# Units of picks that run on from batch to batch, and a clamp of the messages' weights into PSUM, in a graph layer's kernel

## The chip, the cores and the metric

The kernel runs on one core of a Trainium2 chip. The time is device time of one execution, in microseconds; smaller is better. Before the change three runs took 1995.0, 2001.13 and 2002.62 us, with a median of 2001.13. The profile is of another execution, which took 2019.47 us, 2017.7 of them between its first and its last instruction.

## What is computed

One layer of a graph network with residual and normalization. `x` holds 6250 nodes of 64 values, and there are 206250 directed edges, sorted by their destination (the last 6250 by origin are loops).

```python
Qh = (x @ Wq.T + bq).reshape(n, H, D)          # H = 4 heads of D = 16
Kh = (x @ Wk.T + bk).reshape(n, H, D)
Vh = (x @ Wv.T + bv).reshape(n, H, D)
Ee = (edge_attr @ We.T + be).reshape(-1, H, D)
score = (Kh[src] * Qh[dst] * (1.0 / np.sqrt(D)) * Ee).sum(-1)
score = jnp.exp(jnp.clip(score, -5.0, 5.0))
msg = Vh[src] * score[..., None]
wV = jax.ops.segment_sum(msg, dst, num_segments=n)
x = _layernorm(x + wV.reshape(n, H * D), axis=-1)
```

## The kernel before

**Groups and steps.** The edges are cut in 1612 tiles of 128, and eight tiles are a group: 202 groups, whose loop (L1014 to L1139) is the kernel's main part. Two groups are a step. A group passes through stages that lie up to four groups ahead of it in the program:

- `edges(g + 3)`: TensorE multiplies the edges' attributes with We into the PSUM tile `ee`; `biased(g + 2)`: ScalarE adds the bias and makes `eb` in SBUF.
- `onehot_rows` makes one-hot columns of the destinations on ScalarE (`to`); `queries(g + 2)` multiplies them with rows of Q into the PSUM bank `qq`; `terms(g + 1)` is VectorE's product of `eb` and `qq`; `turn(g + 1)` are four transposes on TensorE (L775) into `qe`, of which there are two banks.
- `products(g)`: VectorE multiplies K of the sources with `qe` (`prod`) and reduces to `score`; `weigh(g)`: two ScalarE instructions take the exponential (`weight`); `message(g)`: VectorE multiplies `max(weight, LEAST)` with V of the sources, in one scalar_tensor_tensor (L830), whose product overwrites the group's bank `qe`.
- `keep` and `take` cut the message in two parts for exactness, the one on ScalarE, the other on VectorE (L850). `onehot_edges` (L792) compares destinations with a range, once in a step. `sums` multiplies both on TensorE into the PSUM region `pa`, and `add` (L900 to L909) reduces it on VectorE and adds the result to a ring of blocks. `fold_blocks` and `add_blocks` (L957) bring finished blocks from the ring to `y`.

`ee`, `pa` and `folded` are parts of one PSUM tile of two banks, called `room`; `ee` is its first bank, and the others share its second.

**Gathered and picked sources.** K and V of the sources come from a table in memory, 128 rows at a time, by GpSimd's indirect DMA (L295, 1260 of them). For the last two tiles of some groups, the PICKED ones, TensorE takes the rows of `x` out of `parts`, an SBUF copy of `x`, instead. This goes in 78 batches of four tiles. For a batch, 13 **units** of 512 nodes each run through TensorE: `picks` issues four matmuls a unit into the two banks `px` (tile names pick), with a one-hot tile `hot` that VectorE makes (L696). One-hots are made for two units together, a **piece**; those of pieces 1, 3 and 5 are made in bf16 (`thin`) and widened by ScalarE (`widened`, L707). The sums over units stay in the two banks until the last unit. Then `picked` takes the one wanted row of each four, with two VectorE instructions (L722, L723) that read `odd` (from the loaded `srcs`) and the banks and write `x` in SBUF (`xs`). The first pick of the next batch overwrites the banks, so it has to wait for both. In the next group, `biased_kv` sets the bank `qq` to the bias (ScalarE), `picked_kv` multiplies `x` with the weights of K and V into it (16 matmuls qq<-w,x), and `place_kv` copies it to the gathered rows' places (ScalarE, L739). `queries(g + 2)` of that group uses the same bank and is last in it, after `place_kv`.

**What sets the order.** Each engine runs its instructions in the order in which the loop issues them, and a tile framework adds the waits. Before the change batches take three and two groups by turns (LENGTHS), and `pieces_of` deals the seven pieces of a batch to its groups: 4, 4 and 5 units, or 6 and 7. The last group of a batch is its READY group: 3, 5, 8, 10, 13, and so on. In it, `picked` is the last thing but the closing of blocks. One-hots of a group's units are made in the group before (`ahead`). `sources` (which makes `odd` and the compared numbers from `srcs`) and `fetch_sources` (SyncE's load of `srcs`) run for the next batch at a batch's first group and for the one after in the group ahead.

```python
def picks(m, p, u):
    lo, hi = PIECES[p]
    for k in range(2):
        for part in range(2 if u < UNITS - 1 else 1):
            product(px[k], parts[:, u, part, 2 * k:2 * k + 2].rearrange("p t c -> p (t c)"),
                    HOT[m, p][:, u - lo, :], start=u == 0 and part == 0, stop=u == UNITS - 1)
```

## Time and profile before

| | us | share of the span |
|---|---|---|
| median of three runs | 2001.13 | |
| the profiled execution | 2019.47 | |
| its span | 2017.7 | |
| TensorE busy with matmuls | 1738.5 | 86% |
| VectorE busy | 1486.0 | 74% |
| ScalarE busy | 1328.1 | 66% |
| GpSimd busy | 1255.5 | 62% |
| matmuls of picks (3900) | 1143.6 | 57% |
| DMA, mean rate | 101 GB/s | |

In rows of the profile PE is TensorE, PEld its weight loads, DVE VectorE, ACT ScalarE, POOL GpSimd and SP SyncE. A tile is named by the program, and the number of a line is that of the file before (above). All matmuls but the transposes go through one helper and have its line, L744; they are told apart by the tile that they write. The granted clock of TensorE, in tenths over 40 slices of the span, stands at 9 for the most part, with single slices at 8:

```profile
PEclk9789999999999998999899999999989999999996
```

Busy shares are means over the whole span, start and end among them. They say which engine has the most to do, not which one is waited for; that is read from the waits and the chain.

### The profile page before, as it was taken

What the parts mean: (1) busy time and instruction counts of PE and PEld (TensorE: products, weight loads), DVE (VectorE), ACT (ScalarE), POOL (GpSimd) and SP (SyncE); (2) the same over time, 40 slices, a digit from 0 to 9 for tenths busy, and PEclk for the clock granted to TensorE, in tenths of its full rate; (3) what the DMA queues carried; (4) which work ended last, traced back from release to release, by engine and by line L of the source; (5) the groups of instructions that cost most, each with busy time, mean ns of one, the idle gap of its engine ahead of it and who ended that gap; (6) DMA issues with size and microseconds to landing.
All of it is one profiled execution on the core that took longest, in us unless ns stands there. A gap on an engine that the chain in (4) does not pass through costs nothing.

```text
span 2017.7 us, 25692 instructions
## 1 busy us (share of the span) xinstructions
PE 1738.5 (86%) x7993; PEld 1259.1 (62%) x7993; DVE 1486.0 (74%) x2650; ACT 1328.1 (66%) x2047; POOL 1255.5 (62%) x1310
## 2 busy tenths in 40 slices
PE   6569989888888898979888989888888988889995
PEld 6346666666666665657566666666666666656664
DVE  5457777777777686878777777778777777678786
ACT  3456676676766676767667667667766667577674
POOL 6566666666666665666666666666666666666441
PEclk9789999999999998999899999999989999999996
DMA  6523333333333333333333333333333333333320
GB/s 178 190 90 114 100 103 103 98 97 100 93 108 101 91 102 88 102 115 99 93 97 92 107 104 93 104 90 103 101 88 114 104 95 104 97 93 98 97 71 20
DMA packets 116116, 203.70 MB, mean 101 GB/s; under 512 B 54784, under 2 KB 56425, under 8 KB 115855
## 3 DMA queue, kind: packets, MB, share of 16 engines
q1 hardware_dynamic: 73932, 116.94, 19.0%
q0 software_dynamic: 41600, 83.97, 14.7%
q10 hardware_dynamic: 436, 1.04, 0.2%
q8 instruction: 65, 1.06, 0.2%
q14 instruction: 83, 0.68, 0.1%
HBM read 194.25 MB, written 7.59 MB: 100 GB/s over the span
## 4 chain that ended last, share of the span: by engine, by line
PE 63%; DVE 16%; issue 7%; ACT 6%; another core or an unknown queue 4%; DMA 2%; POOL 1%; DVEq 0%; SPq 0%; ACTq 0%; POOLq 0%
PE pick L744 37%; PE room L744 10%; PE qq L744 10%; PE qe L775 4%; DVE hot L696 3%; DMA kv<-kv_tab,src_i 2%; DVE score L808 2%; DVE prod L806 1%; DVE qe L830 1%; DVE x L722 1%; DVE term L769 1%; POOL kv L295 1%; ACT kv L739 1%; DVE msg L850 1%
## 5 line engine op out<-in xcount | busy, mean ns | idle before, releaser
L295 POOL DMA_INDIRECT kv<-kv_tab,src_i x1260 | 1216.2, 965 | 708.8 <-issue 277.1
L744 PE MATMUL pick<-hot,parts 128*128 128x512 f32 x3900 | 1143.6, 436 | 115.5 <-DVE x L722 79.5
L744 PEld LDWEIGHTS pick<-hot,parts 128*128 128x128 f32 x3900 | 742.3, 198 | 418.8 <-issue 167.8
L696 DVE TENSOR_TENSOR hot<-from,still 128x1024 fp32r<-128x1024 bf16 x231 | 280.3, 1213 | 0.6 <-ACT from L257 0.6
L707 ACT ACTIVATE hot<-thin 128x1024 fp32r<-128x1024 bf16 x234 | 245.4, 1049 | 19.4 <-remote 19.3
L769 DVE TENSOR_TENSOR term<-eb,qq 128x512 f32<-128x512 f32 x202 | 137.3, 680 | 137.2 <-PE qq L744 98.1
L755 ACT ACTIVATE eb<-room,be_col 128x512 f32<-128x512 f32 x202 | 137.1, 679 | 148.2 <-DVE still L900 50.4
L744 PE MATMUL room<-et,we_sb 128*128 128x512 f32 x404 | 226.2, 642 | 7.5 <-ACT eb L755 6.2
L844 ACT ACTIVATE msg<-qe 128x512 fp32r<-128x512 f32 (+1 forms) x206 | 123.2, 598 | 157.5 <-DVE qe L830 74.4
L278 ACT ACTIVATE to<-to,one_p 126x1024 bf16<-126x1024 bf16 x198 | 225.7, 1140 | 0.1
L272 ACT ACTIVATE to<-kb,minus_row 126x1024 bf16<-126x1024 uint8 x198 | 225.2, 1137 | 0.0
L813 ACT ACTIVATE score<-score,five_p 128x32 f32<-128x32 f32 x203 | 64.1, 316 | 235.4 <-DVE score L808 144.6
L775 PE MATMUL qe<-ident,term 128*128 128x128 f32 x806 | 135.5, 294 | 58.9 <-DVE term L769 39.4
L775 PEld LDWEIGHTS qe<-ident,term 128*128 128x128 f32 x806 | 104.0, 151 | 111.9 <-DVE term L769 55.8
L744 PE MATMUL qq<-w,x 128*128 128x128 f32 x1248 | 165.8, 288 | 5.0 <-issue 3.6
L806 DVE TENSOR_TENSOR prod<-kv,qe 128x512 f32<-128x512 f32 x203 | 137.0, 675 | 43.1 <-remote 38.3
L830 DVE SCALAR_TENSOR_TENSOR qe<-weight,kv 128x512 f32<-128x512 f32 x200 | 139.8, 699 | 35.1 <-ACT weight L815 22.3
L722 DVE SCALAR_TENSOR_TENSOR x<-odd,upper,pick 128x512 f32<-128x512 int32 x77 | 57.3, 744 | 144.7 <-PE pick L744 115.2
L744 PEld LDWEIGHTS qq<-w,x 128*128 128x128 f32 x1248 | 155.6, 202 | 12.9 <-issue 8.0
L696 DVE TENSOR_TENSOR thin<-from,still 128x1024 bf16<-128x1024 bf16 x231 | 157.1, 680 | 0.0
L808 DVE TENSOR_REDUCE score<-prod 128x32 f32<-128x512 f32 x203 | 138.5, 682 | 7.0
L850 DVE TENSOR_TENSOR msg<-qe,msg 128x512 fp32r<-128x512 f32 x194 | 132.2, 681 | 2.9 <-ACT msg L844 1.4
(166 smaller groups left out, 1490.5 us busy)
## 6 DMA issues: line engine op xcount, KB each, us to landing
et<-in_eT SPq DMA_DIRECT2D x100, 512.0 KB
kb<-key_tab SPq DMA_DIRECT2D x101, 252.0 KB
kv<-kv_tab,src_i POOLq DMA_INDIRECT x1260
srcs<-in_src_rows SPq DMA_DIRECT2D x78, 256.0 KB
qw<-q_tab SPq DMA_DIRECT2D x202, 15.8 KB
kv_tab<-kv_sb SPq DMA_DIRECT2D x4, 640.0 KB
q_tab<-q SPq DMA_DIRECT2D x5, 480.0 KB
out<-y SPq DMA_DIRECT2D x2, 512.0 KB
```

What stands on the lines that cost most here:

```text
L272: nc.scalar.activation(TO[g][:, :n, :], KB.pop(g)[:, :n * P].rearrange("p (j e) -> p j e", j=n), AF.Square, bias=minus_row3[:3 * W])
L278: nc.scalar.activation(TO[g][:, :n, :], TO[g][:, :n, :], AF.Relu, bias=one_p[:3 * W], scale=-1.0)
L295: return nc.gpsimd.indirect_dma_start(out=kv_of(g)[:, j, :], out_offset=None, in_=kv_tab[:, :], in_offset=bass.IndirectOffsetOnAxis(ap=src ...
L696: nc.vector.tensor_tensor(to.rearrange("p b (a c) -> p b a c", c=2), pairs((FROM if hi < UNITS else OVER)[m])[:, None].to_broadcast(shape) ...
L707: nc.scalar.activation(*THIN.pop(0), AF.Copy)
L744: mark.append(nc.tensor.matmul(*aps, **kw))
L769: nc.vector.tensor_mul(TERM[g][:, :n], EB.pop(g)[:, :n], qq[:, :n])
L775: nc.tensor.transpose(qe[g % 2][:, 2 * k:2 * k + 2, :], TERM[g][:, k, :], ident)
L806: nc.vector.tensor_mul(prod, kv_of(g)[:, lo:hi, :C], qe[g % 2][:, lo:hi, :])
L808: nc.vector.tensor_reduce(SCORE[g], prod.rearrange("p g (h d) -> p g h d", h=H), axis=AX.X, op=OP.add)
L830: nc.vector.scalar_tensor_tensor(to.rearrange("p g (h d) -> p g h d", h=H), WEIGHT.pop(g)[:, :, :, None].to_broadcast([P, n, H, D]), LEAST ...
L850: nc.vector.tensor_sub(part_of(g, 1)[1], left, part)
```

## The change

**Units.** A table FLOW gives the units of each five groups, 4, 6, 6, 4, 6, that is 26, two batches. A batch's units are now one stream, and a READY group has the last units of its batch (`head`, two or five of them) and then the first four or the first one of the next. Where the head is two units, they are issued early in the group, with `picked` right behind them. Where it is five, they come at the usual place, and `picked` follows edges. In both kinds of group `queries`, `sums` and `edges` come between the old batch's last units and the next one's first; `turn` does too in the first kind, and stands behind the second unit in the other. The group after READY has four units always. `sources` and `fetch_sources` run a group earlier.

**Clamp.** `message` is now a tensor_scalar that writes `max(weight, LEAST)` to `least_`, 32 columns of the PSUM bank `still`, and a tensor_tensor that multiplies with it from there.

**The tile room.** `ee` becomes a tile of its own, and `room` keeps `pa` and `folded`.

```diff
+FLOW = 4, 6, 6, 4, 6
+STREAM = [(m, p, u) for m in range(LAST) for p, piece in enumerate(PIECES) for u in range(*piece)]
+UPTO = [0] * (LEAD + 1)
+for g in range(LEAD, NG):
+    UPTO.append(UPTO[-1] + FLOW[(g - LEAD) % len(FLOW)] + (g == LEAD))
...
+def units_of(g):
+
+    return STREAM[UPTO[g]:UPTO[g + 1]] if g < NG else []
...
 def pieces_of(g):
...
+    return [(m, p) for m, p, u in units_of(g) if u == PIECES[p][0]]
...
+SOURCES = {LEAD: 1, **{r: m + 2 for m, r in enumerate(READY)}}
+FETCHES = {r - 1: m + 2 for m, r in enumerate(READY)}
...
-            room = fixed.tile([P, 2, 4 * P], F32, name="room")
-            ee = room[:, 0].rearrange("p (i e) -> p i e", e=P)
-            pa = room[:, 1, :2 * PA]
...
+            ee = fixed.tile([P, G // 2, P], F32, name="ee")
+            room = fixed.tile([P, 4 * P], F32, name="room")
+            pa = room[:, :2 * PA]
...
+            least_ = still[:, 3 * P:3 * P + G * H].rearrange("p (g h) -> p g h", h=H)
...
-                nc.vector.scalar_tensor_tensor(
+                nc.vector.tensor_scalar(least_[:, :n], WEIGHT.pop(g), LEAST, None, op0=OP.max)
+                nc.vector.tensor_tensor(
                     to.rearrange("p g (h d) -> p g h d", h=H),
-                    WEIGHT.pop(g)[:, :, :, None].to_broadcast([P, n, H, D]), LEAST,
+                    least_[:, :n, :, None].to_broadcast([P, n, H, D]),
                     kv_of(g)[:, lo:hi, C:].rearrange("p g (h d) -> p g h d", h=H),
-                    op0=OP.max, op1=OP.mult)
+                    op=OP.mult)
...
-                todo, ahead = [(m, p, u) for m, p in pieces_of(g) for u in range(*PIECES[p])], pieces_of(g + 1)
+                todo, ahead = units_of(g), pieces_of(g + 1)
+                ending = READY.index(g) if g in READY else None
+                head = [one for one in todo if one[0] == ending]
...
                 if g - 1 in FOLDS:
                     add_blocks(FOLDS[g - 1])
+                if 0 < len(head) <= 3:
+                    for one in head:
+                        picks(*one)
+                        where.append(mark[-1])
+                    picked(ending)
                 if g - 1 in READY:
                     biased_kv(READY.index(g - 1))
...
-                for k in range(max(len(todo), 3)):
+                for k, one in enumerate(head if len(head) > 3 else []):
+                    picks(*one)
+                    where.append(mark[-1])
+                    if k == 1 and g + 1 < NG:
+                        turn(g + 1)
+                if head:
+                    if len(head) <= 3 and g + 1 < NG:
+                        turn(g + 1)
+                    if g + 2 < NG:
+                        queries(g + 2)
+                    while short:
+                        short.pop(0)()
+                    if g + 3 < NG:
+                        edges(g + 3)
+                    if len(head) > 3:
+                        picked(ending)
+                    for one in todo[len(head):]:
+                        picks(*one)
+                        where.append(mark[-1])
+                for k in range(0 if head else max(len(todo), 3)):
...
-                if g in READY:
-                    picked(READY.index(g))
```

How this moves instructions is shown at three places, in the order of the program on an engine; a row has the line, the instruction, the tiles (numbers tell buffers apart) and the shape. Lines of the changed kernel are 14 to 16 higher.

**TensorE, around the end of a batch** of three groups (READY group 23). Before: the batch's last picks, the edges' matmul, the first picks of the next batch, and the turn of the next group.

```order
L744 MATMUL pick_757<-hot,parts 128x512
L744 MATMUL pick_758<-hot,parts 128x512
L744 MATMUL room<-et,we_sb 128x512
L744 MATMUL pick_757<-hot,parts 128x512 x2
L744 MATMUL pick_758<-hot,parts 128x512 x2
L744 MATMUL pick_757<-hot,parts 128x512 x2
L744 MATMUL pick_758<-hot,parts 128x512 x2
L775 MATMUL qe_763<-ident,term 128x128 x4
```

After, at the same place:

```order
L759 MATMUL pick_758<-hot,parts 128x512
L759 MATMUL pick_759<-hot,parts 128x512
L790 MATMUL qe_763<-ident,term 128x128 x4
L759 LDWEIGHTS qw
L759 MATMUL qq<-to,qw 64x512
L759 LDWEIGHTS qw
L759 MATMUL qq<-to,qw 64x512
L759 MATMUL ee<-et,we_sb 128x512
L759 MATMUL pick_758<-hot,parts 128x512 x2
L759 MATMUL pick_759<-hot,parts 128x512 x2
```

Between the old batch's last pick and the new one's first stood the edges' matmul alone; now turn and queries stand there too.

**VectorE, in the same group.** Before: from the adding of sums (L900 on) to the products of the next group; L722 and L723 are `picked`.

```order
L900 TENSOR_REDUCE still<-room 64x64 x2
L906 SCALAR_TENSOR_TENSOR ring<-still,above,ring 128x64
L909 TENSOR_SCALAR ring<-still,below 128x64
L696 TENSOR_TENSOR hot<-from,still 128x1024
L830 SCALAR_TENSOR_TENSOR qe_763<-weight,kv_67 128x512
L696 TENSOR_TENSOR thin<-from,still 128x1024
L696 TENSOR_TENSOR hot<-from,still 128x1024
L792 TENSOR_TENSOR of<-still,key 128x1024
L850 TENSOR_TENSOR msg<-qe_763,msg 128x8x64
L722 SCALAR_TENSOR_TENSOR x_759<-odd,upper,pick_757 128x512
L723 SCALAR_TENSOR_TENSOR x_760<-odd,upper_82,pick_758 128x512
L806 TENSOR_TENSOR prod<-kv_68,qe_762 128x512
```

After; L737 and L738 are `picked`, L845 and L846 the message:

```order
L922 SCALAR_TENSOR_TENSOR ring<-still,above,ring 128x64
L925 TENSOR_SCALAR ring<-still,below 128x64
L737 SCALAR_TENSOR_TENSOR x_760<-odd,upper,pick_758 128x512
L738 SCALAR_TENSOR_TENSOR x_761<-odd,upper_82,pick_759 128x512
L711 TENSOR_TENSOR hot<-from,still 128x1024
L845 TENSOR_SCALAR still<-weight 128x32
L846 TENSOR_TENSOR qe_764<-still,kv_67 128x512
L711 TENSOR_TENSOR thin<-from,still 128x1024
L273 TENSOR_SCALAR odd<-srcs 128x512
L807 TENSOR_TENSOR of<-still,key 128x1024
L866 TENSOR_TENSOR msg<-qe_764,msg 128x8x64
L821 TENSOR_TENSOR prod<-kv_68,qe_763 128x512
```

`picked` has moved from behind take to ahead of the group's hot, message, one-hots and take, and the message has become two instructions.

**TensorE, in the group after** (24). Before: what stands between the last of the 16 matmuls of `picked_kv` and `queries`.

```order
L744 MATMUL qq<-w_100,x_760 128x128
L744 MATMUL pick_757<-hot,parts 128x512 x2
L744 MATMUL pick_758<-hot,parts 128x512 x2
L744 MATMUL room<-msg,wide 128x256 x4
L744 MATMUL pick_757<-hot,parts 128x512 x2
L744 MATMUL pick_758<-hot,parts 128x512 x2
L744 MATMUL pick_757<-hot,parts 128x512 x2
L744 MATMUL pick_758<-hot,parts 128x512 x2
L744 MATMUL room<-msg,wide 128x256 x4
L744 MATMUL pick_757<-hot,parts 128x512 x2
L744 MATMUL pick_758<-hot,parts 128x512 x2
L744 LDWEIGHTS qw
```

After:

```order
L759 MATMUL qq<-w_100,x_761 128x128
L759 MATMUL pick_758<-hot,parts 128x512 x2
L759 MATMUL pick_759<-hot,parts 128x512 x2
L759 MATMUL room<-msg,wide 128x256 x4
L759 MATMUL pick_758<-hot,parts 128x512 x2
L759 MATMUL pick_759<-hot,parts 128x512 x2
L759 MATMUL room<-msg,wide 128x256 x4
L759 LDWEIGHTS qw
```

Two units fewer stand between `picked_kv` and `queries` in this group. After a batch of two groups it was two units before as well.

More of the change, by code (lines that the diff above doesn't have):

```diff
@@ L1027, in tile_gnn @@
                     fetch_edges(g // LG + 3, work, 3)
-                if g + 1 in BEGIN[1:]:
-                    fetch_sources(BEGIN.index(g + 1) + 1, work)
+                if g in FETCHES:
+                    fetch_sources(FETCHES[g], work)
                 if g + 4 < NG:
@@ L1096, in tile_gnn @@
                             queries(g + 2)
-                    if k in (2, 4) and short and g not in READY:
+                    if k in (2, 4) and short:
                         short.pop(0)()
@@ L1102, in tile_gnn @@
                     queries(g + 2)
-                if g + 3 < NG:
+                if g + 3 < NG and not head:
                     edges(g + 3)
@@ L1107, in tile_gnn @@
                     onehot_rows_rest(g + 4)
[L1108 to L1109 removed]
+                if g in SOURCES:
+                    sources(SOURCES[g], *from_odd())
                 for i, lot in enumerate(going):
```

11 lines of the change are left out of this document (3 added, 8 removed).

## The prediction

> **What bounds the kernel now.** I read the page's totals and its chain of waits first, then the list of waits with times and counts, then the timeline around one READY group (the last group of a batch), then windows of it.
>
> ```profile
> span 2017.7 us, 25692 instructions
> PE 1738.5 (86%) x7993; PEld 1259.1 (62%) x7993; DVE 1486.0 (74%) x2650; ACT 1328.1 (66%) x2047; POOL 1255.5 (62%) x1310
> PE 63%; DVE 16%; issue 7%; ACT 6%; another core or an unknown queue 4%; DMA 2%; POOL 1%; DVEq 0%; SPq 0%; ACTq 0%; POOLq 0%
> ```
>
> TensorE is busiest and holds 63% of the chain; VectorE follows with 16%. So time goes where TensorE stands, or runs slowly. In the next rows (engine and line, what it waited for, total us, times, longest) stand its waits, and two of other engines:
>
> ```profile
> PE pick L744 <- DVE x L722: 79.5, 23, 6.0
> PE qq L744 <- ACT kv L739: 44.0, 32, 4.4
> PE room L744 <- ACT eb L755: 7.9, 4, 5.6
> DVE x L722 <- PE pick L744: 115.2, 42, 5.1
> DVE x L722 <- remote: 29.5, 7, 6.3
> ACT eb L755 <- DVE still L900: 50.4, 20, 6.5
> ```
>
> The largest is the pick of a new batch, which may not overwrite its two banks until VectorE's two x instructions have read them: 79.5 us in 23 waits, 3.46 us each. The timeline (start, busy us, engine, line) shows one, at the end of a batch:
>
> ```profile
> 998.25 1.02 PE L744 MATMUL room<-et,we_sb 128*128 128x512 f32 x2
> 1000.62 0.68 DVE L792 TENSOR_TENSOR of<-still,key 128x1024 bf16<-128x1024 bf16 x1
> 1001.22 0.68 DVE L850 TENSOR_TENSOR msg<-qe,msg 128x512 fp32r<-128x512 f32 x1
> 1001.82 0.74 DVE L722 SCALAR_TENSOR_TENSOR x<-odd,upper,pick 128x512 f32<-128x512 int32 x1
> 1002.47 0.74 DVE L723 SCALAR_TENSOR_TENSOR x<-odd,upper,pick 128x512 f32<-128x512 int32 x1
> 1002.61 3.78 PE L744 MATMUL pick<-hot,parts 128*128 128x512 f32 x8 [3.34 <-DVE x L722]
> 1006.19 1.05 PE L775 MATMUL qe<-ident,term 128*128 128x128 f32 x4
> 1007.04 2.48 PE L744 MATMUL qq<-w,x 128*128 128x128 f32 x16
> ...
> 979.98 1.96 PE L744 MATMUL qq<-w,x 128*128 128x128 f32 x16
> ...
> 1011.10 2.14 PE L744 MATMUL pick<-hot,parts 128*128 128x512 f32 x8
> 1018.20 0.60 PE L775 MATMUL qe<-ident,term 128*128 128x128 f32 x4
> ```
>
> TensorE ends at 999.27 (998.25 + 1.02) and stands 3.34 us, while VectorE works through one-hots, take and x in its order. Then eight picks take 3.78 us where others take 2.14, the four turns 1.05 against 0.60, the sixteen qq 2.48 against 1.96: 2.6 us more. The windows (stretch; length and PE busy; PEld, DVE, ACT, POOL; granted clock; DMA share; GB/s) say why:
>
> ```profile
> 998.00:1003.00 5.00, 1.66 (x5) 0.77 (x4) 4.97 (x8) 3.98 (x5) 3.78 (x5) 0.83 0.48 156
> 1003.00:1009.00 6.00, 6.00 (x25) 5.08 (x25) 5.97 (x11) 4.98 (x9) 4.48 (x6) 0.57 0.21 64
> 1000.00:1500.00 500.00, 445.24 (x2068) 324.08 (x2069) 377.51 (x650) 340.87 (x512) 323.23 (x335) 0.93 0.34 99
> ```
>
> The granted clock is 0.57 just after the wait and 0.93 over a long stretch. So a long wait of TensorE is paid twice.
>
> **The change part by part.** All sums are made on the profiled execution, 2019.5 us with 2017.7 of span; the median of the runs shown is 2001.1, 18 lower, so I carry the difference over to the median.
>
> *x earlier.* In the 78 READY groups the last two or five units of the ending batch now come first and x stands ahead of one-hots and take on VectorE, while TensorE has other work before the next batch's first pick: turn (0.60), the queries (0.41, below) and edges (1.02), 2.03 us. The two x take 1.39 from 1001.82 to the end of the second (1002.47 + 0.74). In a group whose head is five units, only queries and edges lie between the last old pick and the next new one, 1.43, with sums in some: just enough. So I take the whole wait out: **−79.5**. The clock that follows costs 0 to 2.6 us per wait; not every wait is as long as this one, so I take 1.5, 23 times: **−35** (bounds 0 and −60). [...] What is late next is VectorE: x now waits for the last old picks (115.2 us in 42 waits already), and hot, message, one-hots, take are queued behind it, with sums and x's own readers waiting for those.
>
> *The clamp.* One instruction becomes two: the trace has no clamp into PSUM, so it is bounded by neighbours (mean ns after the busy us):
>
> ```profile
> L830 DVE SCALAR_TENSOR_TENSOR qe<-weight,kv 128x512 f32<-128x512 f32 x200 | 139.8, 699 | 35.1 <-ACT weight L815 22.3
> L909 DVE TENSOR_SCALAR ring<-still,below 128x64 f32<-128x64 f32 x94 | 25.8, 275 | 0.0
> L976 DVE BATCH_NORM_AGGREGATE stats<-six 128x2 f32<-128x6 f32 x49 | 8.9, 182 | 1.7
> L806 DVE TENSOR_TENSOR prod<-kv,qe 128x512 f32<-128x512 f32 x201 | 136.4, 679 | 43.1 <-remote 38.3 <-PE pick L744 2.5 <-issue 0.6
> L609 DVE TENSOR_TENSOR parts<-kv,high 128x512 fp32r<-128x512 f32 x2 | 1.4, 683 | 0.0
> ```
>
> The clamp has 32 elements a partition, between six (182 ns) and 64 (275 ns): 0.25, nearer the 64. The multiply falls from 699 to 679, the row of a multiply with one operand in PSUM, so −0.02, and its dependence on the clamp costs some 0.03. That is 0.26 × 203 messages = 53 us of VectorE's time. On the path it costs its share where VectorE ends last: 16% of it (the chain) is 9, all is 53. VectorE carries more of the path once x moves, so I take **+20** (bounds 0 and +53). A gain below zero is excluded: an instruction is added and the other saves 0.02. If POOL's gathers were freed by it, they would start earlier, but they hold 1% of the chain: by the row below, 1260 of them over 202 groups are 62 per ten groups, at 965 ns 60 us of the 100 that ten groups take (2017.7 / 20.2).
>
> ```profile
> L295 POOL DMA_INDIRECT kv<-kv_tab,src_i x1260 | 1216.2, 965 | 708.8 <-issue 277.1
> ```
>
> [...]
>
> *The tile room split.* Edges' bank and the sums' bank were one tile, so edges waited for the fold of sums, and sums for ACT's eb. TensorE's part is 7.9 us: **−8** (bounds 0 and −16, twice the row, as its clock may fall too). The 50.4 of ACT is off the path (ACT is 66% busy): 0.
>
> *place_kv.* In the group after READY, queries wait for ACT's place_kv, which on ACT stands behind the widened one-hots:
>
> ```profile
> 981.70 2.12 PE L744 MATMUL pick<-hot,parts 128*128 128x512 f32 x8
> 983.62 1.04 ACT L707 ACTIVATE hot<-thin 128x1024 fp32r<-128x1024 bf16 x1
> 984.57 0.65 ACT L739 ACTIVATE kv<-qq 128x256 f32<-128x256 f32 x2
> 985.27 0.41 PE L744 MATMUL qq<-to,qw 126*64 126x512 bf16 x2 [1.46 <-ACT kv L739]
> ```
>
> Today this group has six units after three-group batches and four after the others; it now has four always, so 39 groups lose two units (2.12 us) of cover. The other 39 now build three pieces with two widenings there, 1.04 us more ahead of place_kv. The known total is 44.0 in 32 waits. I take 1.3 us in half of the 39, near today's mean wait (44.0 / 32 = 1.38), 26, since in the other half slack on ACT takes it; and of the widening half, 0.5 us, in 20 of the others, 10: **+36** (bounds 0, and +123 for 39 × 2.12 + 39 × 1.04). Sources (one VectorE instruction a batch) and their loads are issued a group earlier, at nothing: no instruction is added, and SP's queue, which issues the loads, holds 0% of the chain. Without that cover a late load would show as VectorE waiting for srcs.
>
> Sum: −79.5 − 35 + 20 − 8 + 36 = −66.5, that is 1953 on the profiled basis, **1935** on the median's. With the bounds of the unknown terms: best −79.5 − 60 − 16 = −155.5 (1846; clamp and place_kv free), worst, with only x's wait won, −79.5 + 53 + 123 = +96.5 (2098).
>
> **The rivals.**
> *The clock comes back everywhere.* If one wait per ten groups starts the slow passages, most of the lack goes: 7% of 2017.7 is 141 us. Losing 100 of it with the waits 79.5, 29.5 (x <- remote) and 8, less 20 and 36: −161, 1840. For it: the waits recur at one place. Against: the other waits stay and may be the next starters.
>
> *The wait only moves.* x holds up hot, message and one-hots of its own group, so sums and take come later, and VectorE becomes the bound. It is busy in 75% of the long window (377.51 of 500), and I charge both of its additions at that share: x 78 × 1.39 × 0.75 = 81, the clamp 53 × 0.75 = 40, against −79.5 − 35 − 8: −1, **2000**, no change. For it: VectorE is 99% busy in both short windows above (4.97 of 5, 5.97 of 6). Against: over the long window a quarter of its time is free, and the x is moved, not added.
>
> *Slower: place_kv.* With only four units ahead of it, queries wait for place_kv in all 78 groups: today's mean 1.38 plus one widening 1.04, 2.42 × 78 = 189, less the 44 there now: +145. Against it −79.5 − 35 + 20 − 8 = −102.5: +42, **2043**. It decides from a mean wait of (102.5 + 44) / 78 = 1.88 us on. For it: the wait of 1.46 stands already where six units cover it. Against: ACT is 66% busy, so keep and widenings can run ahead.
>
> *The change does not do what it says:* the program's order shows x ahead of the one-hots, so only a wait unseen there could hold x back; 2001.
>
> **How the numbers follow.** A measurement of this kernel tells about 0.5%, 10 us, from no change. The forecast, 1935 with a range of its own from 1885 to 1975, has 0.42; the clock coming back everywhere 0.17; the moved wait 0.19, of which 0.06 comes out faster by more than 10 us (x costs less than its share), 0.11 within and 0.02 above; place_kv 0.20; no effect 0.02. Faster: 0.42 + 0.17 + 0.06 = 0.65; same: 0.11 + 0.02 = 0.13; slower: 0.20 + 0.02 = 0.22. The range has to reach past both signs: from 1845, which takes in half of the first rival and the best sum of the bounds, to 2040, which takes in the moved wait and nearly half of place_kv. That leaves 0.08 out below and 0.10 above; the worst sum lies in the part that is left out.
>
> **What would show it.** Right: pick <- DVE x falls from 79.5 to under 15; granted clock rises from 0.93 to 0.95 or more; room <- ACT eb is gone; the clamp shows near 0.25 us, the multiply near 680; qq <- ACT kv rises from 44 to about 80. Wrong: qq <- ACT kv over 140 (place_kv); the same idle time of TensorE before qe or room and VectorE over 20% of the chain (the wait moved); a clock of 0.98 (the clock came back). A clamp outside 182 to 275 ns would make its term wrong.

## The result, and the profile after

| | median us | lowest to highest, 8 runs each |
|---|---|---|
| before | 1997.8 | 1991.77 to 2005.81 |
| after | 2020.87 | 2008.97 to 2026.63 |

The ratio is 1.010, with a 95% interval of 1.0079 to 1.0122: 1% slower, where 3% faster was forecast. The profiled execution of after took 2021.52 us. That of before (2019.47) lay 22 us above the median of its eight runs, so the two spans, 2017.7 and 2019.4 us, are nearly equal and their difference says nothing. What can be compared is where the engines wait. The page of after, its totals and its chain:

```profile
PE 1721.7 (85%) x7993; PEld 1262.6 (63%) x7993; DVE 1527.8 (76%) x2853; ACT 1327.1 (66%) x2047; POOL 1230.8 (61%) x1310
PE 49%; DVE 18%; ACT 15%; issue 10%; DMA 3%; another core or an unknown queue 3%; POOL 1%; SPq 0%; DVEq 0%; ACTq 0%; POOLq 0%
```

TensorE fell from 63% of the chain to 49%, and ScalarE rose from 6% to 15%. The waits of after say how (engine and line, what it waited for, total us, times, longest):

```profile
PE qq L759 <- ACT kv L754: 52.9, 29, 6.0
PE qe L790 <- DVE term L784: 45.0, 35, 6.2
PE qq L759 <- issue: 25.6, 23, 2.4
PE qq L759 <- ACT qq L748: 21.0, 14, 2.2
PE qq L759 <- ACT weight L830: 13.2, 10, 2.2
PE pick L759 <- DVE x L737: 11.0, 9, 3.2
ACT msg L860 <- DVE qe L846: 182.2, 94, 8.3
ACT msg L860 <- DVE still L845: 51.5, 18, 5.1
PE ee L759 <- ACT eb L770: 10.1, 10, 1.8
```

The same two waits before that the prediction didn't show:

```profile
ACT msg L844 <- DVE qe L830: 74.4, 82, 1.6
PE qe L775 <- DVE term L769: 39.4, 22, 12.3
```

The pick's wait for x is gone, as forecast: 79.5 to 11.0. But ScalarE's keep (msg, L860) now waits 182.2 us for the message instead of 74.4, and 51.5 more for the clamp ahead of it, and TensorE has new waits in front of qq, the bank of queries and of the picked K and V: for its bias (ACT qq, L748), for what ScalarE does ahead of the bias (weight, L830), and 25.6 us for which the profile names no cause ("issue"). The clamp and its multiply, by shape (busy us, mean ns | idle before):

```profile
L845 DVE TENSOR_SCALAR still<-weight 128x32 f32<-128x32 f32 x201 | 39.1, 195 | 52.5 <-ACT weight L830 21.1 <-ACT wide L812 6.9 <-ACT score L828 4.0
L846 DVE TENSOR_TENSOR qe<-still,kv 128x512 f32<-128x512 f32 x200 | 139.8, 699 | 6.8
```

The clamp takes 195 ns, and the multiply 699, as the one instruction before did.

### The profile page after: what moved, and what is told of

It is laid out like the page before. It is cut to its first block, busy times and chain, and to the rows that moved or that the text cites. A ratio compares the mean times of both kernels' runs of the same rounds, so it can differ in the third digit from the quotient of the medians.

```text
span 2019.4 us, 26033 instructions
## 1 busy us (share of the span) xinstructions
PE 1721.7 (85%) x7993; PEld 1262.6 (63%) x7993; DVE 1527.8 (76%) x2853; ACT 1327.1 (66%) x2047; POOL 1230.8 (61%) x1310
## 4 chain that ended last, share of the span: by engine, by line
PE 49%; DVE 18%; ACT 15%; issue 10%; DMA 3%; another core or an unknown queue 3%; POOL 1%; SPq 0%; DVEq 0%; ACTq 0%; POOLq 0%
PE pick L759 26%; PE qq L759 9%; PE ee L759 7%; PE room L759 4%; ACT hot L722 3%; PE qe L790 3%; DVE hot L711 2%; ACT to L286 2%; DVE x L738 2%; ACT to L292 2%; ACT msg L860 2%; DMA qw<-q_tab 2%; DVE score L823 2%; DVE x L737 2%
## 5 line engine op out<-in xcount | busy, mean ns | idle before, releaser
L309 POOL DMA_INDIRECT kv<-kv_tab,src_i x1260 | 1190.8, 945 | 733.8 <-issue 262.4
L759 PE MATMUL pick<-hot,parts 128*128 128x512 f32 x3900 | 1111.5, 430 | 27.0 <-issue 13.9
L860 ACT ACTIVATE msg<-qe 128x512 fp32r<-128x512 f32 (+1 forms) x206 | 123.1, 598 | 296.9 <-DVE qe L846 182.2
L722 ACT ACTIVATE hot<-thin 128x1024 fp32r<-128x1024 bf16 x234 | 245.9, 1051 | 13.0 <-remote 7.6
L759 PE MATMUL ee<-et,we_sb 128*128 128x512 f32 x404 | 234.2, 663 | 10.1 <-ACT eb L770 10.1
L770 ACT ACTIVATE eb<-ee,be_col 128x512 f32<-128x512 f32 x202 | 136.6, 676 | 143.0 <-PE ee L759 51.0
L759 PE MATMUL qq<-w,x 128*128 128x128 f32 x1248 | 182.8, 307 | 54.5 <-ACT qq L748 21.0
L759 PEld LDWEIGHTS qq<-w,x 128*128 128x128 f32 x1248 | 168.0, 216 | 68.9 <-ACT qq L748 25.8
L790 PE MATMUL qe<-ident,term 128*128 128x128 f32 x806 | 129.1, 284 | 71.2 <-DVE term L784 45.0
L790 PEld LDWEIGHTS qe<-ident,term 128*128 128x128 f32 x806 | 98.7, 145 | 121.9 <-DVE term L784 63.5
L737 DVE SCALAR_TENSOR_TENSOR x<-odd,upper,pick 128x512 f32<-128x512 int32 x77 | 57.5, 747 | 135.7 <-PE pick L759 44.2
L759 PE MATMUL qq<-to,qw 126*64 126x512 bf16 x396 | 82.8, 411 | 82.4 <-ACT kv L754 52.9
L846 DVE TENSOR_TENSOR qe<-still,kv 128x512 f32<-128x512 f32 x200 | 139.8, 699 | 6.8
```

The source lines that it names most:

```text
L309: return nc.gpsimd.indirect_dma_start(out=kv_of(g)[:, j, :], out_offset=None, in_=kv_tab[:, :], in_offset=bass.IndirectOffsetOnAxis(ap=src ...
L722: nc.scalar.activation(*THIN.pop(0), AF.Copy)
L759: mark.append(nc.tensor.matmul(*aps, **kw))
L790: nc.tensor.transpose(qe[g % 2][:, 2 * k:2 * k + 2, :], TERM[g][:, k, :], ident)
L846: nc.vector.tensor_tensor(to.rearrange("p g (h d) -> p g h d", h=H), least_[:, :n, :, None].to_broadcast([P, n, H, D]), kv_of(g)[:, lo:hi, ...
L860: nc.scalar.activation(part, left, AF.Copy)
```

## The experiments

The runs were made in six sets, each on a chip of its own, with the kernel before timed beside the others; ratios are to that. The sets differ, which turned out to matter. The kernel before took 2017.7 us in the set of experiments 1 to 4, 2016.8 in that of 5 to 7, 1786.9 in that of 8 and 9, 2002.4 in the first of 10, 1786.7 in one that 10 and 11 share, and 2014.4 in the last, with the second runs of 3 and 11. With 1787 us a set is called one of the faster kind below, with 2000 and more one of the slower kind; the result above is of the slower kind (1997.8).

**1. The clamp undone in the changed kernel.**

```diff
-                nc.vector.tensor_scalar(least_[:, :n], WEIGHT.pop(g), LEAST, None, op0=OP.max)
-                nc.vector.tensor_tensor(
+                nc.vector.scalar_tensor_tensor(
                     to.rearrange("p g (h d) -> p g h d", h=H),
-                    least_[:, :n, :, None].to_broadcast([P, n, H, D]),
+                    WEIGHT.pop(g)[:, :, :, None].to_broadcast([P, n, H, D]), LEAST,
                     kv_of(g)[:, lo:hi, C:].rearrange("p g (h d) -> p g h d", h=H),
-                    op=OP.mult)
+                    op0=OP.max, op1=OP.mult)
```

> The changed kernel with the message of before (one scalar_tensor_tensor from SBUF, no clamp in PSUM). Theory X (the loss sits in the groups that end a three-group batch: x stands ahead of the message on VectorE and waits for TensorE, so ScalarE's keep waits 152 us there instead of 34, and everything behind keep on ScalarE comes late): the clamp is a small part, 2008 to 2021 us, ratio to before 1.005 to 1.01. Theory C (the clamp, 0.195 us of VectorE and its own wait for the weight in each of 203 messages, eats more than the moved x wins): 1990 or less, ratio under 0.997.

2041.1 us, ratio 1.0117 (1.0093 to 1.0141). Without the clamp it is no faster: theory C falls. Theory X has the direction, but the ratio lies above its 1.01.

**2. The clamp alone, in the kernel before.**

> The kernel before with nothing but the clamp into PSUM and the multiply from there. Theory X: the clamp hides mostly in VectorE's free time, 1998 to 2010 us, ratio 1.000 to 1.006. Theory C: 203 x 0.195 = 40 us and a dependent start each, 2018 to 2050 us, ratio 1.01 to 1.025.

2024.7 us, ratio 1.0026 (1.0009 to 1.0043): some 5 us. That is in theory X's range: 39 us of added VectorE time hide almost wholly.

**3. x behind the message.**

```diff
                         picks(*one)
                         where.append(mark[-1])
-                    picked(ending)
...
                     message(g, lo, hi)
+                if 0 < len(head) <= 3:
+                    picked(ending)
```

> The changed kernel with one move: in READY groups whose head is two units the two x instructions are issued behind the message (ahead of keep) instead of ahead of the block of bias, one-hots and message; the units stay where the change puts them. Theory X: keep's wait for the message falls from 152 us towards 34, the new batch's first pick still finds x done, 1980 to 2000 us, ratio 0.99 to 1.00. Theory C: no change from the changed kernel, 2015 to 2027, ratio 1.008 to 1.013.

2037.6 us, ratio 1.0102 (1.0078 to 1.0126), and in a second set 2038.3 us, 1.011 (1.0089 to 1.013):

> The changed kernel with x behind the message but still ahead of one-hots and take. Where signals come in time, the changed kernel had 1.0262 and the one with x behind take 0.9835. If the kernel before takes about 1790 us here: theory X (the message and ScalarE's keep behind x are the price, 144 us of keep's waits against 46) gives 0.98 to 0.995, theory T (one-hots and take behind x are the price) 1.015 to 1.026. If it takes about 2000 us: 1.008 to 1.013 as in the first run of this kernel, and the question stays open.

By its number, theory X was out in the first run (theory C's range has the number, but 1 had taken theory C away), and in the second the question stayed open, as was expected for such a set. The waits show that its mechanism was there and that the time came up again elsewhere. Of the first of these runs:

```profile
PE qq L759 <- ACT kv L754: 94.5, 47, 6.9
PE qe L790 <- DVE term L784: 54.7, 36, 6.2
ACT msg L860 <- DVE qe L846: 112.0, 83, 2.7
```

Keep's wait fell from 182 to 112 us and the bias' wait left TensorE's list, but the queries' wait for place_kv grew from 53 to 95. The move concerns heads of two alone; where the head is five, x still stands ahead of one-hots and take.

**4. The tile room split alone, in the kernel before.**

> The kernel before with the PSUM tile of edges and the tile of sums and folded blocks made separate, and nothing else. Both theories: TensorE's wait room for eb (7.9 us) and part of ScalarE's wait for the reduce (90 us, off the path) go, 1985 to 1998 us, ratio 0.993 to 1.000.

2014.5 us, ratio 0.9978 (0.9962 to 0.9994): 4 us gained, in the range of both theories.

**5. Six units in the group after READY.**

```diff
-FLOW = 4, 6, 6, 4, 6
+FLOW = 6, 4, 4, 6, 6
```

> The changed kernel with the table FLOW 6, 4, 4, 6, 6 in place of 4, 6, 6, 4, 6: the heads stay two and five units, but the group after each READY group has six units instead of four, and the group that is READY with a head of two has two units of the next batch instead of four. Undoing the clamp (1.0117) and moving x behind the message (1.0102) changed nothing, and there the queries' wait for place_kv was 61 and 95 us, against 44 before. Theory K (the loss is the shorter cover of the chain bias, kv matmuls, place_kv, queries on the bank qq in the group after READY): the wait of queries for kv falls under 30 us, ratio to before 0.985 to 1.000. Theory M (TensorE is the follower; what is won at one wait comes up at the next, wherever the units stand): ratio 1.005 to 1.015 as for the changed kernel.

2074.1 us, ratio 1.0277 (1.0249 to 1.0304). Its longest waits of TensorE:

```profile
PE qe L790 <- DVE term L784: 83.1, 49, 6.2
PE pick L759 <- issue: 24.1, 25, 3.2
```

The queries' wait for place_kv is no longer among them, and the kernel lost 1.7% more than the changed one (1.010): the turn now waits longer. The wait of queries is thus no cause that can be taken away by itself; theory K falls, and the ratio lies above theory M's 1.015 as well. K falls in the next run too.

**6. place_kv first on ScalarE,** with the row one-hots and the second widening behind it in the group after READY.

> The changed kernel with one reordering on ScalarE: in the group after READY the one-hots of rows (two instructions of 1.14 us) and the second widening (1.05 us) are issued behind place_kv instead of ahead of it. Theory K: place_kv comes up to 2 to 3 us earlier in these 78 groups, the queries' wait for kv falls under 25 us, ratio to before 0.990 to 1.003. Theory M, or if place_kv is late because of its matmuls and not of ScalarE's queue: ratio 1.005 to 1.013, kv wait as in the changed kernel.

2036.8 us, ratio 1.010 (1.0083 to 1.0117), as theory M had it: no gain. The queries' wait for kv, which M had as in the changed kernel, rose from 52.9 to 71.7 us.

**7. x ahead of one-hots and take, in the kernel before.**

```diff
                 if g + 3 < NG:
                     edges(g + 3)
                 where.append(mark[-1])
+                if g in READY:
+                    picked(READY.index(g))
...
-                if g in READY:
-                    picked(READY.index(g))
```

> The kernel before with one move: the two x instructions of a READY group are issued right behind its edges, ahead of sources, one-hots and take on VectorE; units, message and PSUM tiles as before. Theory K (moving x is good, the changed table of units is what costs): the pick's wait for x falls from some 80 us by about 23 x 1.2 = 28 us and a part of the slow clock with it, ratio 0.980 to 0.995. Theory M: the time comes up again at turn (waiting for term) and at queries (waiting for kv), ratio 0.997 to 1.005.

2043.3 us, ratio 1.0151 (1.0128 to 1.0175), above both theories' ranges. This is one step of the change without the rest of it, as the change makes it where the head is five, and it costs 1.5%; where the head is two the change moves x further, ahead of hot and message. Its waits:

```profile
DVE x L722 <- PE pick L744: 136.8, 43, 5.2
DVE x L722 <- remote: 62.8, 13, 6.7
PE pick L744 <- DVE x L722: 62.0, 15, 5.6
PE qe L775 <- DVE term L769: 56.6, 28, 5.3
```

The pick's wait for x fell from 79.5 to 62.0 only, while VectorE's waits at x rose from 145 us (115.2 + 29.5) to 200, and turn waits longer for term. A reading that fits, though this run alone doesn't show it, is that one-hots and take had filled time in which x had to wait for the last picks anyway. There is more to see in the timeline of one such wait (start, busy us, engine, line):

```profile
1055.77 2.60 PE L744 MATMUL pick<-hot,parts 128*128 128x512 f32 x10
...
1059.16 1.02 PE L744 MATMUL room<-et,we_sb 128*128 128x512 f32 x2
...
1063.63 0.75 DVE L722 SCALAR_TENSOR_TENSOR x<-odd,upper,pick 128x512 f32<-128x512 int32 x1 [5.37 <-remote]
1063.75 0.94 POOL L295 DMA_INDIRECT kv<-kv_tab,src_i  x1 [2.44 <-remote]
...
1064.43 3.78 PE L744 MATMUL pick<-hot,parts 128*128 128x512 f32 x8 [4.25 <-DVE x L722]
```

By the record the last picks that x waits for end at 1058.37 (1055.77 + 2.60), and TensorE's very last matmul at 1060.18. GpSimd's gather of 1060.36 ends at 1061.30; from there to 1063.63 TensorE, VectorE and GpSimd all stand. VectorE and GpSimd start within 0.12 us of each other, 3.4 us after TensorE's last work, and SyncE's load of `et` follows at 1063.82. In the trace all three wait on one semaphore, the one that TensorE counts up; its records there stand at 1062.06 and, eight of them, between 1063.49 and 1063.80. The profile puts such a wait down to "remote", another core or an unknown queue; the program has one core. As these records have it, what is late is the signal that TensorE's work is complete: it comes 5.3 us after the end of the last picks (the ends of matmuls are modelled).

**8. x behind one-hots and take, in the changed kernel.** TensorE's order stays as changed.

```diff
                         picks(*one)
                         where.append(mark[-1])
-                    picked(ending)
...
                     if g + 3 < NG:
                         edges(g + 3)
-                    if len(head) > 3:
-                        picked(ending)
+                    if g + 4 < NG:
+                        onehot_rows_rest(g + 4)
+                    onehots(g)
+                    if parted:
+                        take(g, 0)
+                    picked(ending)
                     for one in todo[len(head):]:
                         picks(*one)
```

`onehots` holds what the loop issued further down for all groups; there it and `take` now run for the other groups alone.

> The changed kernel with x back behind the one-hots and take on VectorE in both kinds of READY group (onehot_edges, take, then x, then the picks of the next batch); TensorE's order, with turn, queries, sums and edges between the old batch's last unit and the next one's first, stays as the change makes it. Moving x ahead of them in the kernel before cost 1.5% (1.0151), although TensorE's wait for x fell. Theory W (VectorE runs in order and x has to wait for TensorE's last picks; whatever stands behind x is late by that, so x ahead of one-hots and take is what costs, and the other parts of the change gain): VectorE's idle time at x falls from 136 us to under 100, TensorE's wait for x stays under 60, ratio to before 0.985 to 0.998. Theory S (the loss is in the table of units and the earlier turn, queries and edges, wherever x stands): 1.006 to 1.02.

1756.4 us against 1786.9 of the kernel before, ratio 0.9835 (0.9821 to 0.9848): 1.65% faster than before, a little more than theory W's 1.5%, with both waits as W said (13.7 and 29.4 us, below). It is some 4% below the ratio of the changed kernel in the other set of the faster kind (1.0262, under 10). Its trace has no wait on "remote" at all.

**9. Half of the picks left out, in the kernel before,** in the same set.

> The kernel before with one of the two parts of each pick left out (the second half of the split of x is not added): 1950 of 3900 pick matmuls, some 570 us of TensorE's 1738. Theory B (TensorE bounds the kernel, as the chain of waits with 63% says): 300 us or more of them come off the time, ratio under 0.85. Theory L (a ring of waits through the three engines bounds each group, and picks fill TensorE's time in it): less than 160 us, ratio 0.92 to 0.98.

1698.6 us, ratio 0.9503 (0.9485 to 0.9521). Half of the pick matmuls give 5% of the time, 88 us, as theory L had it; theory B falls. The totals of its trace:

```profile
PE 1369.2 (81%) x6121; PEld 959.3 (56%) x6121; DVE 1478.7 (87%) x2650; ACT 1319.4 (78%) x2047; POOL 1254.0 (74%) x1310
```

TensorE's granted clock was 0.88 in these runs, against 0.98 of the kernel before beside them, so the matmuls that are left ran slower (in the trace of 7 eight picks take 2.15 us at a granted clock of 1.00 and 3.78 at 0.50). The run shows that after 88 us something other than TensorE's work holds the time. It doesn't show that TensorE's work holds none of it in the whole kernel, since 88 us is more than the 66.5 us that were forecast; that a ring of waits through the engines sets the time is argued.

**10. The same kernels in other sets.** The changed kernel, x behind take, the kernel before, and x ahead of one-hots, in one set:

> The changed kernel itself, beside the kernel before. The kernel before took some 1998 us beside the changed one, 2017 beside the first seven experiments, and 1787 beside the last two; in the traces of those two no consumer of TensorE's results started late, while in all others results were signalled up to 5 us after the end of their matmul (26 holes of TensorE with such a burst in the trace of the changed kernel, 25 before). Theory N (where signals come in time, the change gains as forecast; the late signals take the gain back, since the change puts more readers close behind TensorE): if the kernel before takes about 1790 us here, ratio 0.975 to 0.992; if it takes about 2000, 1.006 to 1.013 again. Theory W (x ahead of one-hots and take costs, wherever it runs): 1.00 to 1.015 in either case.

> The changed kernel with x back behind the one-hots and take (ratio 0.9835 where the kernel before took 1787 us). Theory N: with the kernel before at about 1790 us, 0.980 to 0.987 again and within 0.5% of the changed kernel; at about 2000 us, 1.00 to 1.015. Theory W: 0.98 to 0.99 in either case, and better than the changed kernel by 1% or more.

> The kernel before, for a profile beside the others of this call: 1787 us with no late signals, or 2000 to 2020 us with some 25 holes that end in a burst of them.

> The kernel before with x moved ahead of one-hots and take, nothing else (1.0151 where the kernel before took 2017 us). Theory N: with the kernel before at about 1790 us, 0.99 to 1.00; at about 2000 us, 1.01 to 1.02 again. Theory W: 1.01 or more in either case.

Before 2002.4; changed 2023.2, ratio 1.0113 (1.0077 to 1.0148); x behind take 2036.8, ratio 1.0184 (1.016 to 1.0208); x ahead of one-hots 2032.3, ratio 1.0163 (1.014 to 1.0187). The one kernel that had gained 1.65% now lost 1.84%, outside the ranges of both theories: here x behind one-hots and take is no better place. The other two ratios lie in the ranges of both. Then the changed kernel fell in a set of the faster kind:

> The changed kernel once more, beside the kernel before and the two without gathers. Theory N: ratio 1.006 to 1.015 if the kernel before takes about 2000 us here, 0.975 to 0.992 if it takes about 1790. Theory W: 1.00 to 1.015 in either case.

1832.1 us, ratio 1.0262 (1.0245 to 1.0279), a greater loss than either theory had. Theory N, that the change gains where signals are in time, falls. Theory W has the direction: with x behind one-hots and take the same kernel goes from 1.0262 to 0.9835, in two sets of the faster kind. A place in the changed kernel, around a READY group with a head of two, without any late signal:

```profile
791.04 0.32 ACT L830 ACTIVATE weight<-score,five_p 128x32 f32<-128x32 f32 x1
794.47 0.75 DVE L737 SCALAR_TENSOR_TENSOR x<-odd,upper,pick 128x512 f32<-128x512 int32 x1 [1.80 <-PE pick L759]
795.13 0.74 DVE L738 SCALAR_TENSOR_TENSOR x<-odd,upper,pick 128x512 f32<-128x512 int32 x1
795.79 1.21 DVE L711 TENSOR_TENSOR hot<-from,still 128x1024 fp32r<-128x1024 bf16 x1
797.34 0.70 DVE L846 TENSOR_TENSOR qe<-still,kv 128x512 f32<-128x512 f32 x1
798.07 0.60 ACT L860 ACTIVATE msg<-qe 128x512 fp32r<-128x512 f32 x1 [4.08 <-DVE qe L846]
...
804.34 0.58 ACT L748 ACTIVATE qq<-bkv_all 128x512 f32<-128x512 f32 x1
804.97 3.22 PE L759 MATMUL qq<-w,x 128*128 128x128 f32 x16 [2.20 <-ACT qq L748]
```

The weight is there at 791.36, but VectorE stands 1.80 us at x for the last picks, and the message's multiply starts at 797.34, behind x and a one-hot. Keep stands for 4.08 us, and with it ScalarE's queue: the bias of the next group comes 6.27 us after keep's start, and TensorE waits 2.20 us for it at qq. The same group with x behind take:

```profile
765.97 0.32 ACT L844 ACTIVATE weight<-score,five_p 128x32 f32<-128x32 f32 x1
769.06 0.70 DVE L860 TENSOR_TENSOR qe<-still,kv 128x512 f32<-128x512 f32 x1
769.79 0.60 ACT L874 ACTIVATE msg<-qe 128x512 fp32r<-128x512 f32 x1 [0.87 <-DVE qe L860]
771.46 0.73 DVE L737 SCALAR_TENSOR_TENSOR x<-odd,upper,pick 128x512 f32<-128x512 int32 x1
772.25 6.08 PE L759 MATMUL pick<-hot,parts 128*128 128x512 f32 x24 [0.82 <-DVE x L737]
776.06 0.58 ACT L748 ACTIVATE qq<-bkv_all 128x512 f32<-128x512 f32 x1
778.60 1.95 PE L759 MATMUL qq<-w,x 128*128 128x128 f32 x16
```

Keep waits 0.87, x runs without waiting, and TensorE pays 0.82 for it. The bias comes 6.27 us after keep here too, but in time, and the sixteen matmuls take 1.95 us, not 3.22: after the wait of 2.20 the granted clock is 0.62 over 4.5 us, and at the same place without the wait it is 1.00. Over the whole run the changed kernel has

```profile
DVE x L737 <- PE pick L759: 80.8, 71, 2.6
PE qe L790 <- DVE term L784: 56.6, 37, 6.2
PE qq L759 <- ACT qq L748: 41.5, 32, 2.2
PE qq L759 <- ACT kv L754: 37.0, 35, 2.0
```

and x behind take

```profile
PE qe L790 <- DVE term L784: 31.8, 15, 6.2
PE pick L759 <- DVE x L737: 29.4, 25, 2.8
PE qq L759 <- ACT kv L754: 24.0, 25, 1.6
DVE x L737 <- PE pick L759: 13.7, 15, 1.2
PE qq L759 <- ACT qq L748: 3.0, 13, 0.3
```

TensorE's three waits for term, bias and kv add up to 135 us in the changed kernel; with 29 us spent on x again they are 59. Which of the instructions behind x carries most of it, message or one-hots and take, was not separated by a run of the faster kind: run 3 fell both times in a set of the slower kind. The two traces say where the time goes. The turn of one group starts at 142.06 us in the changed kernel and at 142.19 with x behind take; 188 groups later it starts at 1784.13 and 1708.65, so 75.6 us are lost in between. From the turn of a READY group with a head of two to that of the next READY group it is 26 us in all, and from the turn of one with a head of five to that of the next 50. In groups of the second kind the message stands ahead of x in both kernels; what stands behind x is one-hots and take. These sums are net of what x costs TensorE at its later place, and a delay of one group can show in the next.

**11. The gathers left out,** from group 1 of the loop on, in the kernel before and in the changed one.

```diff
-                for i, lot in enumerate(going):
+                for i, lot in enumerate(going if g == 0 else []):
                     gather((lot, where[i * len(where) // len(going)]))
```

> The kernel before without the gathers of K and V from group 1 of the loop on (about 1200 of 1260 indirect DMAs are left out; sources' rows are those of the first steps). Theory G (the gathers' transfers and their completion signals hold up TensorE's signals): no hole of TensorE ends in a late burst, and the time is that of the good chip or less, 1700 to 1790 us, also where the kernel before takes 2000. Theory O (something else of the chip holds them up): late bursts stay, 1930 to 2000 us where the kernel before takes 2000.

> The changed kernel without the same gathers. Theory N (the change gains where signals come in time) with G: 1 to 2.5% faster than g1, 1665 to 1765 us. Theory N with O: 0.5 to 1.5% slower than g1 where signals are still late. Theory W (x ahead of the one-hots costs in itself): as fast as g1 or up to 1% slower in either case.

> The kernel before without the gathers from group 1 on, which took 1782 us where the kernel before took 1787. If the kernel before takes about 2000 us here: theory G (the gathers hold up TensorE's signals) gives 1700 to 1800 us and no late bursts, theory O (something else of the chip does) 1930 to 2000 with late bursts. If it takes about 1790: 1782 again, and the question stays open.

Beside a kernel before of 1786.7 us, the one without gathers took 1782.5, ratio 0.9974 (0.9964 to 0.9984), and the changed one 1820.2, ratio 1.0204 (1.0166 to 1.0242). The changed kernel is thus 2.1% slower than the kernel before without gathers as well, outside the ranges of both theories N and W. Beside one of 2014.4 us, the same kernel before without gathers took 1806.4, ratio 0.8956 (0.8933 to 0.8978), far from theory O's range and just above theory G's 1800. Where signals are in time the gathers cost 0.3%; elsewhere 10%. The late signals go with them. The kernel before with gathers, in the set of 2002.4 us, had among its waits

```profile
POOL kv L295 <- remote: 51.1, 26, 4.0
DVE x L722 <- remote: 29.4, 6, 6.1
ACT kv L739 <- remote: 22.4, 8, 4.8
DVE term L769 <- remote: 15.6, 2, 11.4
```

and without gathers none of these four is left: the largest wait on "remote" in it is

```profile
ACT eb L755 <- remote: 13.3, 2, 9.3
```

In that trace the last wait on "remote" ends at 115.63 us, 1.8 us after the start of the last gather that is kept (113.86). The granted clock rises with them, from between 0.927 and 0.941 to between 0.976 and 0.980. Theory G holds but for its bound of 1800 us. How a gather delays the signal of a matmul these runs don't show, nor whether it is the gathers' work on GpSimd or the traffic that they make.

## Why the prediction was wrong

**What bounds the kernel.** The first wrong step was to take "time goes where TensorE stands, or runs slowly" as if a wait of TensorE that goes were time gained. In the pair of one set (10) the pick's wait for x fell from 84.7 to 9.1 us, but TensorE's idle time, the span less its busy time, rose from 279.0 to 287.3. A share of 63% in the chain doesn't say how much of an engine's work or waiting can be taken out before something else binds; with half of the picks left out it was 88 us (9), in a set of the faster kind.

**x earlier, −79.5.** The wait went as said, 79.5 to 11.0. What failed is the sum: the prediction named what stands behind x on VectorE ("hot, message, one-hots, take are queued behind it") and charged nothing for it. On the faster kind that price is the result: undone in 8, it takes the ratio from 1.0262 to 0.9835. On the slower kind, that of the result, x ahead of one-hots and take costs 1.5 to 1.6% alone (7 and 10, in two sets), but putting x back in the changed kernel doesn't help (1.0184), nor does x behind the message (1.0102): there the loss isn't owed to one place, what the late signals add to each was not separated, and its cause stays open.

**The clock, −35.** It brought no time. In the first set of 10 the granted clock is a little higher with the change (0.940 to 0.953, against 0.934 to 0.942 before), but TensorE's busy time in the profiled pair is 1726.2 us after 1719.7. On the faster kind the clock is lower with the change, 0.965 to 0.968 against 0.980 to 0.984: the new wait at qq brings a slow passage of its own, as shown under 10.

**The clamp, +20.** Its instruction was placed rightly between 182 and 275 ns (195), and the multiply starts 34 ns after the clamp's end, near the 0.03 us charged. The multiply gained nothing: 699 ns with the clamp in PSUM and 699 before with both sources in SBUF, though in another instruction, not 679. Alone the clamp costs 5 us (2). The term was mis-sized: +20 for some 5.

**The tile room, −8.** 4 us alone (4): right in kind, half the size. In the changed kernel the wait that it was to remove is not gone but stands at the new tile, 10.1 us of ee for eb.

**place_kv, +36.** The queries' wait for kv rose from 44.0 to 52.9, 9 us, not 36. What the prediction didn't have is the bias ahead of it, 21.0 us, with 13.2 more for weight and 25.6 under "issue" in front of the same bank. Bias and weight follow from keep standing behind x: with x behind the message (3) the first falls to 0.4 us and the second is gone. The 25.6 fall to 16.4 there, and the changed kernel of the faster kind has no such row, so they belong with the late signals more likely than with keep. So the rival "slower: place_kv" didn't win either; widening the cover took its wait away and made the kernel slower still (5).

**The rivals.** "The wait only moves" came nearest, mechanism and place: x holds up hot, message and one-hots of its own group. It was priced at 2000 on the grounds that a quarter of VectorE's time is free, with 0.02 for slower. But free time at other places didn't help the message that stands behind x, for which ScalarE waited 4.08 us at the place shown under 10; and keep, with all of ScalarE behind it, was left out of that price. The signs that were to show this rival didn't come: VectorE's share of the chain is 18%, under the 20 named, and the wait before qe went only from 39.4 to 45.0. The share that rose was ScalarE's, for which there was no sign. The prediction also read past a row: 29.5 us of x waiting on "remote" in a program on one core was used as a lump for one rival and not followed up; such a row stands in the trace of the kernel before in the set of 2002.4 us as well (29.4 us), and x has none in the traces of the faster kind shown above or in that without gathers.

## What to carry to other kernels

When an instruction is moved forward on an engine that runs in order, price what it passes: if it has to wait for another engine, all that it passed waits with it, and so do their readers on the third engine. Here VectorE stood 1.80 us at x, and ScalarE's keep 4.08 us for the message behind it (10). A wait of the busiest engine that disappears need not be time gained: here one fell from 84.7 to 9.1 us while that engine's idle time rose from 279.0 to 287.3. Leave out part of that engine's work once, and see how much of it comes off the time. And time a kernel with many gathers on more than one chip before one version is preferred: here the ratio of one version to the kernel before turned from 0.9835 to 1.0184.

## What the runs showed of the hardware

The same program, the kernel before, took 1787 us in two sets and 1998 to 2018 in the five others (the result among them), 12% apart, with its repeats in a set within 1% of each other. The six sets of the experiments were on six chips, each used once, so whether it is the chip or the time of the set that makes the kind was not separated. In the place shown of a trace of the slower kind (7) TensorE's completion signal comes 5.3 us after the end of the last picks by their record; in three traces of the faster kind, of the changed kernel, of x behind take and of the kernel before without gathers, no reader waits on "remote". The granted clock of the kernel before is 0.980 to 0.984 on the faster kind and 0.926 to 0.943 on the slower. Leaving out the gathers brings the slower kind to 1806 us (0.8956), and the clock to 0.976 to 0.980, and leaves the faster nearly as it is (0.9974); so the lower clock goes with the gathers and isn't owed to the chip alone.

The traces of the slower kind also hold fewer records of semaphores, for all three engines. The kernel before in the set of 2002.4 us has 1283 records for the 2456 times that VectorE's instructions count one up, 949 for ScalarE's 1816 and 1728 for TensorE's 2167; the changed kernel of the faster kind has 2598 for 2600, 1722 for 1722 and 2401 for 2405. So the names of what ended a wait are less sure on the slower kind, and that TensorE's signals alone are late there isn't shown.

The best version found is the changed kernel with x behind one-hots and take (1756 us), on the faster kind alone; on the slower kind only the split of the tile room gained, by 0.2%, with the gathers in place.
